# Moving the order of work inside a fused attention and FFN kernel: first pair's sums, next x's second half, y's turn, one maximum, one pair's statistics

## The chip, the cores and the metric

The kernel runs on one core of a Trainium2 chip. The metric is device time in microseconds (us). A core has five engines that run beside each other, each in the order in which its instructions were written: TensorE (PE in the profile, with its weight loads as PEld), VectorE (DVE), ScalarE (ACT), GpSimd (POOL) and SyncE (SP), which here only issues transfers. An engine that waits for something holds up all that stands behind it in its own list.

## The reference

Eight items (B = 8) of 1024 rows and 256 columns pass through one block. `mod` holds six rows for each item, and the two gates are kept away from zero.

```python
h = layernorm(x) * (1 + ca) + sa
x = x + ga * attention(h)            # softmax(h*w_lhs @ (h*w_rhs).T) @ h
h = layernorm(x) * (1 + cb) + sb
x = x + gb * (relu(h @ W1 + b1) @ W2 + b2)
```

All of it is float32. The scores of an item are symmetric (each is a sum over columns of x, x and both weights), so the kernel computes those on and above the diagonal and turns the rest.

## The kernel before, in words

The outer loop runs over items `b`, the inner one over eight steps `i`; step i belongs to row tile i of 128 rows. While attention runs for item b, the FFN of item b - 1 is interleaved: half 0 (`fg` = 0) in steps 0 to 3, half 1 in steps 4 to 7. A half has 512 rows. Its first matmuls are taken in four "pairs" c = 0 to 3, two in steps 0 and 1 (4 and 5) each, its second matmuls in steps 2 and 3 (6 and 7). Both products are done by a Strassen-like scheme with seven products instead of eight, so there are sums before and after them on DVE and POOL. `pin` (L63) ties each engine to the order in which the program was written: a statement's place in the loop is its place in every engine's list. DMAs are issued from SP's list, but for the loads of x and of two rows, which are issued from ACT's.

What each step issues, as far as the change touches it:

- `direct` (L403) makes the scores of row tile i + 2 on PE, copied to `sc` by ACT; `mirror` (L424) turns them on DVE (`Tm`), writes them to HBM in four transfers (`D_m`) and reads them back into `sc` as the columns of the later tiles (`move`, L300). `row_max` (L461, DVE, reads all of a tile's scores) gives `m`; `max_turn` (L466, PE) spreads it as `pm`; `subtract` (L471, DVE) and `exponent` (L483, ACT) make `pT`.
- Two row tiles form a pair. `left_sums` (L563) makes four sums on POOL. `pair_begin` (L539) issues products on PE and a copy to `W` on ACT (one buffer), `pair_end` (L574) twenty more products, and `pair_out` (L594) eight instructions on DVE that read the PSUM tiles `pq` and `pr` and write x. `pair_stats` (L620) takes the two tiles' statistics.
- `pair_products` (L723) issues the FFN's first products `pa`, `pb`, `pc` and the ACT copy `kept`; `between` is called behind them. `pair_sums` (L749) is five DVE instructions (L757 to L767), `pair_last` (L769) one product, one DVE add (L775) and one POOL add (L776), `pair_relu` (L780) two ACT instructions, `pair_turn` (L787) four POOL instructions that make `ft`.
- `y_first` (L803) issues `ya` and `yb`. Their first halves read `f`; then ACT copies `ya` to the tile `Y` (L811, one buffer), and the second half of `ya` follows on PE and reads `ft[:, 1]` of all four pairs. `y_second` (L825) issues `yc` and `yd`. `y_gate` scales Y on ACT, `y_turn` (L855) turns it with two DVE transposes (L860), writes four transfers `D_y` and leaves the reading back for later: the next `move` that is in a hurry or `y_add` (L868) issues it. `y_add` is two POOL adds (L873) of Y to x, and `y_out` (L875) writes x.
- `ffn_norm` (L643, ACT into `X_f`), `ffn_blocks` (L676, two DVE transposes, `D_f`, read back into X) and `ffn_turn` (L682) make the FFN's input `hT` and its sums `hs` on POOL.
- For the next item: `load_x`, `prepare_stats` (DVE), `prepare_rstd` (two ACT instructions), `prepare_norm` (one DVE, four ACT), `prepare_blocks` (two DVE transposes, `D_a`, read back into the single buffer `X`), `prepare_turn_apart` (L336, two ACT instructions for each side). `x_plus` and `xg_times` only append POOL work to a queue, which `spare()` takes from in steps 2, 3, 6 and 7.

In step 4 the order is: `direct`, `pair_begin`, pair 0 of the FFN with `max_turn` of tile 5 behind its products, `subtract` of tile 5, `y_turn`, `mirror` of tile 6, `pair_last`, pair 1 with `exponent` and `left_sums`, `prepare_norm` and `prepare_blocks` of the next item's second half, then `row_max` of tile 6. In step 5 pair 2 follows, with `max_turn` of tile 6 behind its products, then pair 3, `subtract` of tile 6, `y_add` and two `pair_turn`.

Of the kernel before, what the change touches and what calls it, by code (L numbers as in the profile page):

```python
# [24 lines left out]
def adaln_block_kernel(  # L25
# [14 lines left out]
    B, S, D = x.shape  # L40
# [228 lines left out]
    def prepare_rstd(b, g):  # L269
        pre[b, g].append(rstd_of(pre[b, g][0], "ra", f"ra_{b}_{g}"))  # L270
# [195 lines left out]
    def max_turn(b, i):  # L466
        pm = ps_t.tile([P, HALF], F32, tag="t", name=f"pm_{b}_{i}")
        nc.tensor.transpose(pm[:, :P], max_t.pop((b, i)).to_broadcast([P, P]), ident)
        pT_t[b, i] = pm
# [194 lines left out]
    def x_plus(b, g):  # L664

        for t in range(g * TH, (g + 1) * TH):
            xr = x_tile(b, t)
            later(xr, xr, rows_t[b][:, 1, :], ALU.add)
# [54 lines left out]
    def pair_products(b, g, c, between=None):  # L723

        if c == 0:
            ffn["f"] = two.tile([P, NI, HALF], F32, tag="f", name=f"f_{b}_{g}", bufs=1)
            if b < B - 1:
                ffn["ft"] = two.tile([P, 3, NH, H2], F32, tag="ft", name=f"ft_{b}_{g}", bufs=1)
        hT, hs = ffn["hT", g]
        n = ts(c, P)  # L730
        s1, a22 = (w1[:, k, ds((c + NH) * P, P)] for k in range(2))

        pool, tag = (ps_s, "s") if b == B - 1 else (ps_a, "a")
        pa = ps_a.tile([P, HALF], F32, tag="a", name=f"pa_{b}_{g}_{c}")
        pb = pool.tile([P, HALF], F32, tag=tag, name=f"pb_{b}_{g}_{c}")
        pc = ps_a.tile([P, HALF], F32, tag="a", name=f"pc_{b}_{g}_{c}")
        mm(pa[:, lo], w1[:, 0, n], hT[:, 0, lo])
        mm(pa[:, hi], s1, hs[:, 0])

        tag, bufs = ("s1", 1) if b == B - 1 and c % 3 == 2 else ("kept", 2)  # L740
        kept = work.tile([P, HALF], F32, tag=tag, name=f"kept_{b}_{g}_{c}", bufs=bufs)
        nc.scalar.copy(kept, pa)  # L742
        mm(pb[:, lo], w1s[:, 0, n], hs[:, 1])
        mm(pb[:, hi], w1s[:, 1, n], hs[:, 2])
        mm(pc[:, lo], w1[:, 1, n], hT[:, 1, lo])
        mm(pc[:, hi], a22, hT[:, 0, hi])
        if between:
            between()
        pairs[c] = pa, pb, pc, kept  # L749
# [387 lines left out]
    def weights(b, i):  # L1137
        subtract(b, i)
        exponent(b, i)
# [3 lines left out]
    for b in range(B):  # L1143
        for i in range(NT):
# [6 lines left out]
            c = i % TH * 2  # L1151
# [56 lines left out]
            if first:  # L1208

                ub, ug = (b - 1, 0) if i >= TH else (b - 2, 1)  # L1210
                back = i % TH == 0 and ub >= 0
                returned = i % TH == 1 and ub >= 0
                if i == 4:
                    pair_begin(b, i)
                    pair_begin_sum(b, i)
                pair_products(fb, fg, c, turn_max)
                if i == 0:
                    ffn_rstd(b - 1, 1)
                if back:
                    y_gate(ub)  # L1220
                if i == 4:
                    if b + 1 < B:
                        prepare_rstd(b + 1, 1)
                if i % TH == 1:
                    pair_relu(c - 1)
                pair_sums(fb, fg, c)
                if (b, i) == (1, 0):
                    subtract(*late)
                elif i == 4:
                    subtract(*late)  # L1230
                if back:
                    y_turn(ub, ug)
                if ahead:
                    mirror(*ahead)
                if i == 1:
                    left_sums(b, 0)
                pair_last(fb, fg, c)
                if i % TH == 1:
                    pair_turn(c - 1)
                if (b, i) == (B - 1, 5):  # L1240
                    pair_stats(b, 2)
                pair_products(fb, fg, c + 1, (lambda: max_turn(*extra)) if extra else None)
                if (b, i) == (1, 0):
                    exponent(*late)
                    late = None
                if (b, i) == (B - 1, 5):
                    ffn_rstd(b, 0)
                if i == 4:
                    exponent(*late)
                    left_sums(b, i)  # L1250
                    if b + 1 < B:
                        prepare_norm(b + 1, 1)
                        x_plus(b + 1, 1)
                pair_relu(c)
                pair_sums(fb, fg, c + 1)
                pair_last(fb, fg, c + 1)
                if i == 0:
                    pair_begin(b, i)
                if late and i != 4:
                    weights(*late)  # L1260
                if i == 5 and b + 1 < B:
                    prepare_turn_apart(b + 1, 1, 1)
                    prepare_turn_apart(b + 1, 1, 0)
                middle(b, i)
                if i == 4 and b + 1 < B:
                    prepare_blocks(b + 1, 1)
                    xg_times(b + 1, 1)
                if ahead and ahead != extra:
                    row_max(*ahead)
                if returned:  # L1270
                    for q in range(2):
                        y_add(ub, ug, q)
                pair_turn(c)
                if c > 0:
                    pair_relu(c + 1)
                    pair_turn(c + 1)
            else:
                half = i % TH - 2
                if i == NT - 2 and b < B - 1:
                    pair_stats(b, 2)  # L1280
                if i == 2:
                    pair_begin(b, i)
                elif i == 3:
                    turn_max()
                elif i == 6:
                    pair_begin(b, i, lambda: (max_turn(*late), weights(*late)))
                else:
                    turn_max()
                    pair_end(b, i - 1)
                    if not ahead:  # L1290

                        pair_out(b, i - 1)
                        pair_stats(b, i - 1)
                if half:
                    y_second(fb, fg)
                else:
                    y_first(fb, fg, turn_max if i == 2 else None)
                if ahead:
                    mirror(*ahead)
                if i == 2 and b + 1 < B:  # L1300
                    prepare_rstd(b + 1, 0)
                elif i == 6 and b + 1 < B:
                    ffn_rstd(b, 0)
                elif i == NT - 1 and b == B - 1:
                    ffn_rstd(b, 1)
                if not half:
                    pair_begin_sum(b, i)
                    if i == 2:
                        weights(*late)
                    left_sums(b, i)  # L1310
                spare()
                early(b, i)
                if late and half:
                    weights(*late)
                middle(b, i)
                if i == 2 and b + 1 < B:
                    load_x(b + 1, 1)
                spare()
                if ahead:
                    row_max(*ahead)  # L1320
                if half:
                    if i == NT - 1 and ahead:
                        pair_out(b, i - 1)
                    y_second_sums(fb)
                    if i == NT - 1 and b == B - 1:
                        y_gate(fb)
                    elif i == 3:
                        pair_stats(b, 0)
                        if b + 1 < B:
                            prepare_stats(b + 1, 1)  # L1330
                else:
                    y_first_sums()
                    if i == NT - 2:
                        pair_stats(b, 4)
                spare()
            if extra:
                subtract(*extra)
            if i == NT - 1 and 0 < b < B - 1:
                while queue:
                    spare()  # L1340
                right_sums(b + 1, range(4))
            turns(b, i)
            norms(b, i)
            if extra:
# [3 lines left out]
                    spare()  # L1348
            if i == 0:
                pair_begin_sum(b, i)  # L1350
            elif i in (1, 3, 5):
                pair_end(b, i - 1)
                pair_out(b, i - 1)
                if i == 3 and b + 1 < B:
                    prepare_turn_apart(b + 1, 0, 1)
                    prepare_turn_apart(b + 1, 0, 0)
            elif i == NT - 1 and ahead:
                pair_stats(b, i - 1)
            late = ahead if ahead != extra else None
# [82 lines left out]
```

## Time and profile before

| | |
|---|---|
| three runs | 801.06, 804.87, 805.19 us, median 804.87 us |
| the profiled execution: its time, its span | 801.43 us, 799.3 us |
| mean granted TensorE clock | 0.996 |
| PE busy, share of the span | 758.0 us, 95% |
| DVE | 621.5 us, 78% |
| POOL | 577.4 us, 72% |
| ACT | 377.5 us, 47% |

The 2.1 us between time and span lie around the instructions. The view of waits lists, for an engine, which earlier instruction ended its idle time, with the total, the number of times and the longest. The timeline gives the start of a group of like instructions in us from the span's start, its length, engine, line, operation, operands and count, and in brackets the idle time before it and what ended it; a letter q behind the engine marks an issue of its queue. One item takes some 96 us; item 4's steps 4 to 7 lie at about 411 to 460 us.

### The profile page before, as it was taken

How to read it: one execution, taken by the hardware profiler on the slowest of the kernel's cores; microseconds unless marked ns; L12 is line 12 of the kernel's file. 1: busy time of each engine (PE TensorE's matmuls, PEld its weight loads, DVE VectorE, ACT ScalarE, POOL GpSimd, SP SyncE). 2: the span in 40 equal slices, each digit the busy share in tenths (PEclk: the TensorE clock that was granted, in tenths of full speed). 3: DMA queues.
4: the chain of work that ended last, by engine and by line, in shares of the span. 5: the costliest groups of instructions: out<-in, count | busy, mean ns of one | idle time of the engine just before them, and what ended most of it. 6: DMA issues, size and time to landing. Idle time of an engine off the chain costs nothing.

```text
span 799.3 us, 12434 instructions
## 1 busy us (share of the span) xinstructions
PE 758.0 (95%) x4044; PEld 624.8 (78%) x4044; DVE 621.5 (78%) x1358; ACT 377.5 (47%) x695; POOL 577.4 (72%) x686
## 2 busy tenths in 40 slices
PE   8999998999989999899998999989998999998998
PEld 4687876787867788687796877868877788877887
DVE  7896789778896887867888688877779868785833
ACT  4563536534455445544455355553546535243421
POOL 3854876969779597885869968688686987758730
PEclk9999999999999999999999999999999999999999
DMA  8033253344533444434534444335452443424130
GB/s 291 14 107 112 73 159 92 103 135 133 165 113 114 124 140 132 124 113 124 158 103 139 145 125 142 100 110 145 132 164 71 125 123 112 113 60 146 43 115 27
DMA packets 106217, 95.25 MB, mean 119 GB/s; under 512 B 29701, under 2 KB 98849, under 8 KB 106153
## 3 DMA queue, kind: packets, MB, share of 16 engines
q1 hardware_dynamic: 98408, 85.81, 36.6%
q10 hardware_dynamic: 7744, 8.65, 3.5%
q8 instruction: 32, 0.52, 0.3%
q14 instruction: 33, 0.26, 0.1%
HBM read 50.62 MB, written 43.81 MB: 118 GB/s over the span
## 4 chain that ended last, share of the span: by engine, by line
PE 71%; DVE 19%; issue 3%; ACT 3%; DMA 3%; DVEq 0%; SPq 0%; ACTq 0%
PE psc L412 13%; PE pr L588 7%; PE pa L721 6%; PE yc L799 6%; PE pb L721 5%; PE ya L799 5%; PE pq L588 5%; PE yb L799 5%; PE pp L549 4%; PE po L501 3%; PE py L909 3%; PE yd L799 3%; PE pc L721 3%; DVE u L767 2%; ACT X_f L653 2%
## 5 line engine op out<-in xcount | busy, mean ns | idle before, releaser
L412 PE MATMUL psc<-rT,lT 128*128 128x512 f32 (+3 forms) x384 | 134.8, 487 | 0.0
L484 ACT ACTIVATE pT<-pT 128x1024 f32<-128x1024 f32 x64 | 67.8, 1059 | 114.2 <-DVE pT L475 114.2
L776 POOL TENSOR_TENSOR f<-f,kept 128x256 f32<-128x256 f32 x64 | 49.3, 771 | 95.3 <-DVE f L766 74.4
L475 DVE TENSOR_TENSOR pT<-sc,pm 128x1024 f32<-128x1024 f32 x64 | 77.6, 1213 | 34.4 <-DMA sc<-D_m 19.7
L412 PEld LDWEIGHTS psc<-rT,lT 128*128 128x128 f32 x384 | 66.4, 191 | 37.3 <-issue 25.3
L463 DVE TENSOR_REDUCE m<-sc 128x1 f32<-128x1024 f32 x64 | 77.3, 1207 | 2.3 <-ACT sc L419 1.7
L419 ACT COPY sc<-psc 128x512 f32<-128x512 f32 (+3 forms) x96 | 44.1, 473 | 72.7 <-PE psc L412 58.6
L721 PE MATMUL pb<-hs,w1s 128*128 128x256 f32 x256 | 68.1, 390 | 3.1 <-DVE f L760 3.1
L721 PE MATMUL pc<-hT,w 128*128 128x256 f32 x256 | 66.9, 384 | 0.0
L549 PEld LDWEIGHTS pp<-xg,pT 128*128 128x128 f32 x448 | 54.3, 192 | 10.5 <-issue 4.8
L742 ACT COPY kept<-pa 128x512 f32<-128x512 f32 x64 | 37.5, 586 | 52.6 <-PE pa L721 52.5
L567 POOL TENSOR_TENSOR s<-pT 128x512 f32<-128x512 f32 x28 | 35.6, 1270 | 33.4 <-ACT pT L484 33.4
L588 PE MATMUL pq<-tsum,pT 128*128 128x128 f32 (+1 forms) x448 | 59.3, 275 | 0.3 <-DVE f L760 0.3
L721 PEld LDWEIGHTS pb<-hs,w1s 128*128 128x128 f32 x256 | 48.8, 194 | 12.7 <-DVE f L760 5.7
L549 PE MATMUL pp<-xg,pT 128*128 128x129 f32 x448 | 56.1, 277 | 1.0 <-ACT pT L484 0.2
L721 PEld LDWEIGHTS pc<-hT,w 128*128 128x128 f32 x256 | 49.6, 194 | 7.1
L757 DVE SCALAR_TENSOR_TENSOR u<-pb,cols,kept 128x256 f32<-128x256 f32 x64 | 30.4, 475 | 31.6 <-PE pb L721 26.4
L588 PEld LDWEIGHTS pq<-tsum,pT 128*128 128x128 f32 x448 | 54.5, 192 | 0.5 <-DVE f L760 0.5
L637 POOL TENSOR_TENSOR x<-x,rows 128x256 f32<-128x256 f32 x64 | 44.5, 726 | 12.7 <-ACT rows L1015 9.6
L782 ACT ACTIVATE f<-f 128x512 f32<-128x512 f32 x64 | 40.2, 628 | 22.7 <-DVE f L775 22.7
L799 PE MATMUL yc<-f,w2s 128*128 128x256 f32 x224 | 50.7, 379 | 0.0
L783 ACT ACTIVATE f<-f 128x512 f32<-128x512 f32 x64 | 39.7, 621 | 17.4 <-POOL f L776 17.3
(167 smaller groups left out, 1931.8 us busy)
## 6 DMA issues: line engine op xcount, KB each, us to landing
D_f<-T_f SPq DMA_DIRECT2D x60, 128.0 KB, 2.3
X_f<-D_f SPq DMA_DIRECT2D x15, 512.0 KB, 3.8
D_a<-T_a SPq DMA_DIRECT2D x56, 128.0 KB, 2.8
D_y<-T_y SPq DMA_DIRECT2D x56, 128.0 KB, 2.3
Y<-D_y SPq DMA_DIRECT2D x14, 512.0 KB, 4.3
out_dram<-x SPq DMA_DIRECT2D x14, 512.0 KB, 3.0
X_a<-D_a SPq DMA_DIRECT2D x13, 512.0 KB, 3.4
x<-in_L_attn_x_dram ACTq DMA_DIRECT2D x12, 512.0 KB, 3.8
```

What stands on the lines that cost most here:

```text
L412: nc.tensor.matmul(psc[:, : hi - lo], lhsT=lT_t[b, i // TH][:, k, ts(i % TH, P)], rhs=rT_t[b, n][:, k, lo - n * HALF : HALF], start=(k == ...
L419: nc.scalar.copy(score_row(b, i)[:, lo // V : hi // V, :], psc[:, : hi - lo].rearrange("p (n v) -> p n v", v=V),)
L463: nc.vector.tensor_reduce(m, score_row(b, i), AX.XY, ALU.max)
L475: nc.vector.tensor_tensor(pT.rearrange("p j (a v) -> p j a v", v=V), score_columns(b, i), pm[:, :P].rearrange("p (j a v) -> p j a v", j=1, ...
L484: nc.scalar.activation(pT_t[b, i], pT_t[b, i], AF.Exp)
L549: nc.tensor.matmul(out, lhsT=lhs[:, t, :], rhs=xg_t[b][:, h * TH + t, P : P + XS], start=(t == 0), stop=(t == TH - 1),)
L588: nc.tensor.matmul(out, lhsT=lhs[:, t, :], rhs=rhs[:, t, :], start=(t == 0), stop=(t == TH - 1),)
L637: queue.append(lambda: nc.gpsimd.tensor_tensor(out, in0, row, op))
L721: nc.tensor.matmul(out, lhsT=lhsT, rhs=rhs, start=True, stop=True)
L776: nc.gpsimd.tensor_tensor(f[:, c + NH, hi], f[:, c + NH, hi], kept[:, hi], ALU.add)
L782: nc.scalar.activation(f[:, c, :], f[:, c, :], AF.Relu)
L799: nc.tensor.matmul(out, lhsT=lhs(c), rhs=rhs(c), start=(c == 0), stop=(c == NH - 1))
```

## The change

The diff moves calls inside the loop; no function's body changes. In step 1 `pair_end` and `pair_out` of the first pair stand in front of `turns` and `norms` instead of behind them (`norms` of step 1 issues `ffn_blocks`, `prepare_start` and `prepare_stats`). The next item's second half has its statistics, `prepare_rstd`, `prepare_norm`, `x_plus`, `prepare_blocks` and `xg_times` in step 3 instead of steps 3 and 4, its `load_x` in step 2 ahead of `prepare_norm` of the first half; `prepare_turn_apart` of the first half stays in step 3 and now stands ahead of these blocks. The y of steps 4 and 5 is turned in step 5, behind `subtract` and `exponent` of tile 6; that of steps 0 and 1 is left where it was. The maximum of tile 6 is spread behind pair 3's products instead of pair 2's. `pair_stats` of the first pair goes from step 3 to step 6, but for the last item.

```diff
--- before.py
+++ after.py
@@ -1213,14 +1213,11 @@
                 if i == 4:
                     pair_begin(b, i)
                     pair_begin_sum(b, i)
-                pair_products(fb, fg, c, turn_max)
+                pair_products(fb, fg, c, turn_max if i != 5 else None)
                 if i == 0:
                     ffn_rstd(b - 1, 1)
                 if back:
                     y_gate(ub)
-                if i == 4:
-                    if b + 1 < B:
-                        prepare_rstd(b + 1, 1)
                 if i % TH == 1:
                     pair_relu(c - 1)
                 pair_sums(fb, fg, c)
@@ -1228,7 +1225,7 @@
                     subtract(*late)
                 elif i == 4:
                     subtract(*late)
-                if back:
+                if back and i == 0:
                     y_turn(ub, ug)
                 if ahead:
                     mirror(*ahead)
@@ -1239,7 +1236,10 @@
                     pair_turn(c - 1)
                 if (b, i) == (B - 1, 5):
                     pair_stats(b, 2)
-                pair_products(fb, fg, c + 1, (lambda: max_turn(*extra)) if extra else None)
+                pair_products(
+                    fb, fg, c + 1,
+                    turn_max if i == 5 else (lambda: max_turn(*extra)) if extra else None,
+                )
                 if (b, i) == (1, 0):
                     exponent(*late)
                     late = None
@@ -1248,9 +1248,6 @@
                 if i == 4:
                     exponent(*late)
                     left_sums(b, i)
-                    if b + 1 < B:
-                        prepare_norm(b + 1, 1)
-                        x_plus(b + 1, 1)
                 pair_relu(c)
                 pair_sums(fb, fg, c + 1)
                 pair_last(fb, fg, c + 1)
@@ -1258,13 +1255,12 @@
                     pair_begin(b, i)
                 if late and i != 4:
                     weights(*late)
+                if i == 5:
+                    y_turn(ub, ug)
                 if i == 5 and b + 1 < B:
                     prepare_turn_apart(b + 1, 1, 1)
                     prepare_turn_apart(b + 1, 1, 0)
                 middle(b, i)
-                if i == 4 and b + 1 < B:
-                    prepare_blocks(b + 1, 1)
-                    xg_times(b + 1, 1)
                 if ahead and ahead != extra:
                     row_max(*ahead)
                 if returned:
@@ -1295,8 +1291,13 @@
                     y_second(fb, fg)
                 else:
                     y_first(fb, fg, turn_max if i == 2 else None)
+                if i == 6 and b + 1 < B:
+                    pair_stats(b, 0)
                 if ahead:
                     mirror(*ahead)
+                if i == 3 and b + 1 < B:
+                    prepare_stats(b + 1, 1)
+                    prepare_rstd(b + 1, 1)
                 if i == 2 and b + 1 < B:
                     prepare_rstd(b + 1, 0)
                 elif i == 6 and b + 1 < B:
@@ -1308,13 +1309,16 @@
                     if i == 2:
                         weights(*late)
                     left_sums(b, i)
+                if i == 2 and b + 1 < B:
+                    load_x(b + 1, 1)
                 spare()
                 early(b, i)
                 if late and half:
                     weights(*late)
+                if i == 3 and b + 1 < B:
+                    prepare_norm(b + 1, 1)
+                    x_plus(b + 1, 1)
                 middle(b, i)
-                if i == 2 and b + 1 < B:
-                    load_x(b + 1, 1)
                 spare()
                 if ahead:
                     row_max(*ahead)
@@ -1325,9 +1329,13 @@
                     if i == NT - 1 and b == B - 1:
                         y_gate(fb)
                     elif i == 3:
-                        pair_stats(b, 0)
                         if b + 1 < B:
-                            prepare_stats(b + 1, 1)
+                            prepare_turn_apart(b + 1, 0, 1)
+                            prepare_turn_apart(b + 1, 0, 0)
+                            prepare_blocks(b + 1, 1)
+                            xg_times(b + 1, 1)
+                        else:
+                            pair_stats(b, 0)
                 else:
                     y_first_sums()
                     if i == NT - 2:
@@ -1339,6 +1347,9 @@
                 while queue:
                     spare()
                 right_sums(b + 1, range(4))
+            if i == 1:
+                pair_end(b, 0)
+                pair_out(b, 0)
             turns(b, i)
             norms(b, i)
             if extra:
@@ -1348,12 +1359,9 @@
                     spare()
             if i == 0:
                 pair_begin_sum(b, i)
-            elif i in (1, 3, 5):
+            elif i in (3, 5):
                 pair_end(b, i - 1)
                 pair_out(b, i - 1)
-                if i == 3 and b + 1 < B:
-                    prepare_turn_apart(b + 1, 0, 1)
-                    prepare_turn_apart(b + 1, 0, 0)
             elif i == NT - 1 and ahead:
                 pair_stats(b, i - 1)
             late = ahead if ahead != extra else None
```

## The prediction

> **What bounds the kernel now.** I read the page first (PE 95% busy, all others at 78% or less), then what PE waits for, then the timeline of item 4's steps 4 to 6, engine by engine. In the view of waits the five costliest rows of PE, from 40 us on, are
>
> ```profile
> PE pm L468 <- DVE m L463: 18.6, 7, 2.9
> PE yb L799 <- DVE pr L606: 7.0, 7, 1.7
> PE pb L721 <- DVE f L760: 3.1, 6, 0.5
> PE ya L799 <- ACT Y L811: 2.8, 2, 2.6
> PE pa L721 <- DVE f L775: 2.4, 7, 0.5
> ```
>
> Their sum, 33.9 us, is the most that any reordering can win: 4.2% of the span, some 5 us of an item's 96. Two places in an item carry it. In the timeline of PE they are, step 5 first and step 2 of the next item second:
>
> ```profile
> 420.22 0.70 PE L721 MATMUL pa<-hT,w 128*128 128x256 f32 x2 [0.41 <-DVE f L775]
> 421.87 1.13 PE L721 MATMUL pb<-hs,w1s 128*128 128x256 f32 x4 [0.52 <-DVE f L760]
> 426.76 0.32 PE L468 MATMUL pm<-ident,m 128*128 128x128 f32 x1 [2.90 <-DVE m L463]
> ...
> 489.91 1.99 PE L799 MATMUL yb<-f,w 128*128 128x256 f32 x8 [0.98 <-DVE pr L606]
> ```
>
> In step 5 DVE is late: from 415.2 to 434.4 it is never idle, and these three of its rows stand in front of tile 6's maximum:
>
> ```profile
> 418.36 1.29 DVE L860 STREAM_TRANSPOSE T_y<-Y 128x512 f32<-128x512 f32 x2
> 420.09 0.81 DVE L277 SCALAR_TENSOR_TENSOR rs<-mva,ra 128x4 f32<-128x4 f32 x1
> 424.31 1.29 DVE L322 STREAM_TRANSPOSE T_a<-xg 128x512 f32<-128x512 f32 x2
> ```
>
> **First pair's sums earlier: -1.5 us an item.** In item 4's step 2, `yb` waits for L606, since `pair_out` began at 392.42, behind T_f (389.09, after 1.40 idle) and four pairs of statistics (2.1). Moved ahead, it starts when the maximum ends (387.7) and `pair_end`'s last product is through (387.4), and ends 2.7 later at 390.4. `yb` then follows `ya` at 390.72 + 1.73 = 392.45, not 393.60, and the second half of `ya` starts at 394.3, not 395.79: L811 was queued behind the copy to W, which waited 4.63 for `pair_out` and now doesn't. Together 1.5. The price: T_f ends 1.3 later, and its X_f read goes to SP at 395.35, not 394.04; `y_out` and tile 4's mirror stand behind it, so its writes start at 396.2, not 395.63. hT has its cover until pair 0 in step 4.
>
> **Next x's second half earlier, a pair's statistics later.** From step 4 go one small DVE row (0.7 in place), T_a (1.2) and four ACT rows (2.1). Into step 3 come the same; there DVE idled 1.81 ahead of `subtract` of tile 4, and the 2.1 of x's statistics fill that gap. `pair_stats` (1.06) leaves step 3 and lands in step 6 behind `subtract` of tile 7, where DVE idled 1.19 at the next mirror. `load_x` now stands on ACT ahead of the four `prepare_norm`, and its buffer must have been written out: `y_out` at 395.75 plus 3.0 (its median landing) is 398.8, so ACT stands 2 us. That keeps T_a of step 2 where it was in absolute time (about 401). The D_a transfers move past tile 6's mirror, into a stretch in which SP idled from 411.1 to 419.7; POOL's queued x and xg rows are the same eight and still run in steps 6 and 7. I cost this at nothing by itself. Bounds: -0.5 an item if DVE reaches pair 0 earlier, +0.7 if the x load slows the mirror's transfers.
>
> What it does to `subtract` of tile 5 (417.23), where the next chain begins: `subtract` of tile 4 waits for its mirror, 404.44 + 0.6 = 405.0. Then 1.15 for it, 1.05 exponent, 2.1 for four norms, 1.25 T_a, 2.7 `pair_out`, 0.85 for W and `kept`, 2.05 for five sums: 416.15. So of the 1.5 gained, 1.1 arrives.
>
> **Maximum and y later: the stall of 3.8 goes.** Without T_y, T_a and the small row in front of it, tile 6's maximum ends near 421.8, and its `pm` is now asked for behind pair 3's products, near 424.8. 2.90 + 0.52 + 0.41 = 3.83 goes. All that stands between is 3 us of cover.
>
> **What is late next.** `y_turn` now stands behind `subtract` of tile 6, and `y_add` in the same step needs its data back from HBM. Before, Y was asked for at 426.12 and the adds ran at 433.37 without a wait; these are POOL's rows, and everything under L873 is queued behind it:
>
> ```profile
> 424.96 0.72 POOL L776 TENSOR_TENSOR f<-f,kept 128x256 f32<-128x256 f32 x1
> ...
> 432.69 0.73 POOL L776 TENSOR_TENSOR f<-f,kept 128x256 f32<-128x256 f32 x1
> 433.37 2.51 POOL L873 TENSOR_TENSOR x<-x,Y 128x512 f32<-128x512 f32 x2
> ...
> 439.35 0.73 POOL L792 TENSOR_TENSOR ft<-f 128x256 f32<-128x256 f32 x1 [0.48 <-ACT f L783]
> 440.16 0.73 POOL L793 TENSOR_TENSOR ft<-ft,f 128x256 f32<-128x256 f32 x1
> ```
>
> PE's second half of `ya` (443.63) needs the last of these. From `subtract` of tile 5 I count: POOL's L776 of pair 1 ends 8.45 later (425.68 - 417.23; exponent and four left sums are in it). ACT's second relu of pair 1 waits for that, and `kept` of pair 3 is behind it: 1.15. Five sums and L775 of pair 3: 2.6 (429.40 to 431.98). `subtract` of tile 6: 1.13. T_y: 1.3. Its transfers: the shortest stretches from the first of four writes to the read's issue are 3.6 to 3.7 (390.43 to 394.04, 725.23 to 728.95), and from a read to its first user 3.4 to 3.6 (X_a 431.89 to 435.31, 406.29 to 409.85); I take 7.0. `y_add` 2.5, `pair_turn` of pair 2 3.05, two rows of pair 3's 1.55, PE's last two records 0.45. Sum 29.2: the second half of `ya` would end at 416.15 + 29.2 = 445.35. Before it ended at 443.63 + 1.73 = 445.36.
>
> So POOL stands idle some 6 us where it had no wait, PE waits there in turn, and the 5.3 gained is paid back: without new waits `ya` would end at 440.0. L811, too, must wait for `y_add`, since Y has one buffer (about 440.3); `load_x` behind it on ACT waits for `y_out` (near 443.5), and `ffn_norm` starts about when it did (444.29), so X_f and hT are covered as before. `left_sums` of tile 6's pair start about 4 later and end 451.8; `pair_end` needs the last of them near 453.9. Per item: 0.0, for six items nothing.
>
> **The last item** prepares nothing, so less was late: PE waited 1.18 + 0.26 in step 5. The same sum from 705.8 (its old 705.94: the mirror's 0.6 eats the 1.5) goes through DVE, which was the later there: T_y ends at 720.6, Y is back at 727.6, `ya` ends at 727.6 + 2.5 + 3.05 + 1.55 + 0.45 = 735.15 instead of 732.62. Its left sums then end 1.1 too late for `pair_end`: +3.6.
>
> **The clock.** After the 2.90 of items 3 and 5 the granted clock was 0.50 and four `pb` records took 1.91 instead of 1.03; after item 4's it stayed at 1.00. From step 4's `pair_begin` to the next item's those two stretches took 97.8 instead of 96.3: 3.0 in all. They go. The new wait has a longest gap of 2.4 (between the two pair_turns); at two in six or fewer I charge one such loss, 1.5.
>
> The Trainium skill, "TensorE: Matmul & The Clock Gate", section "Why this matters for your kernels", advises no idle gaps over some 3 us, as one idle window drops the clock to half. The rows show the drop after 2.90. By the page the new gap is safe, and the sum would be 1.5 lower.
>
> **Sum.** 0.0 + 3.6 - 3.0 + 1.5 = +2.1 on the profiled execution's 801.43. That lies 3.4 below the median of 804.87; on the median it is 807.0, and I say 807: nothing that can be told.
>
> The skill's "DMA: Bandwidth & Descriptors", section "Anatomy of one DMA", would put a transfer at 2.0 us plus bytes over 436 GB/s. My estimate by that page for 128 KB and 512 KB is 2.3 + 3.2 = 5.5, not the rows' 7.0; seven items would then gain 10 and the time would be 797.
>
> **Rivals.** *Faster*: the chain from `subtract` of tile 5 is shorter than 29.2. The tile arrives at PE's pace (415.7: -0.45), the transfers at the shortest rows (6.9: -0.1), DVE's rows unstretched beside an idle POOL (-0.6): -1.2 an item, -8 in seven, 799. It is decided by Y's add starting before 437.5 in item 4's frame; every us earlier is worth 7, until at -5.3 an item all stalls are gone (770), for which no row speaks.
>
> *Slower*: Y comes back later, and each us costs 7. The one place where y was asked for at once, in the tail, speaks for it:
>
> ```profile
> 757.66 1.98 SPq L306 DMA_DIRECT2D D_y<-T_y  x4
> 762.29 0.34 SPq L309 DMA_DIRECT2D Y<-D_y  x1
> ...
> 765.60 2.49 POOL L873 TENSOR_TENSOR x<-x,Y 128x512 f32<-128x512 f32 x2 [5.70 <-DMA Y<-D_y]
> ```
>
> 7.94 instead of 7.0, beside another read; with 0.7 for the x load against the mirror, +1.6 an item, 818. It decides from an add after 438.5. Against it: no other transfer is issued in that stretch.
>
> *Nothing moved*: tile 6's maximum is still last, or PE's gain of step 2 alone is left: 803 to 807.
>
> **Chances.** Forecast 0.45 (803 to 811; 0.28 of it within half a per cent, 0.16 slower, 0.01 faster). Faster rival 0.32 (0.29 and 0.03 within). Slower rival 0.19. Nothing moved 0.04. Half a per cent, 4 us, is what a measurement can tell from no change. So faster 0.30, same 0.35, slower 0.35. The range, 794 to 818, leaves out some 0.1 at each end.
>
> **What would show it.** PE's waits for m and for L606 gone from the list; a new wait of PE's `ya` for POOL's `ft` or ACT's Y, 4 to 5 us an item; a wait of L873 for Y of some 6; ACT standing at `load_x`. If `ya` of step 6 does not wait, the step "what is late next" is wrong, and the time is under 790. If `pm` still waits, the cover of 3 us is.

## The result, and the profile after

The changed kernel took 826.07 us in the median of four runs (825.37 to 827.8), the kernel before 803.93 (801.06 to 805.19, four runs): a ratio of 1.0284, 95% interval 1.025 to 1.0318. The change costs 22 us. The forecast was 807.0 with a range of 794 to 818, so it is outside, on the slow side. The profiled execution took 825.37 us, 1.8 of them around its span. Of its page, the span, the engines' busy time and the shares of the chain that ended last:

```profile
span 823.6 us, 12454 instructions
...
PE 768.8 (93%) x4044; PEld 624.6 (76%) x4044; DVE 620.1 (75%) x1358; ACT 378.6 (46%) x695; POOL 579.4 (70%) x686
...
PE 36%; DVE 22%; POOL 18%; DMA 13%; issue 6%; ACT 3%; SPq 1%; DVEq 0%; POOLq 0%; ACTq 0%
```

DVE, POOL and ACT have no more to do than before (DVE 620.1 against 621.5 us, POOL 579.4 against 577.4). PE has the same 4044 records and is busy 10.8 us longer: by the record of the granted clock 17.1 us lie at half the clock, before 6.8, and a record behind a wait takes longer (two records of `ya` 0.70 us, without a wait 0.59). PE's waits from 40 us on grow from 34.4 to 47.7 us. What is new is the chain: before it ran through PE for 71% of the span, now for 36%, and POOL and transfers have 31%. What PE waits for, from 40 us on (total, times, longest):

```profile
PE ya L799 <- POOL ft L793: 14.9, 7, 2.3
PE ya L799 <- ACT Y L811: 9.9, 7, 4.0
PE pa L721 <- ACT kept L742: 8.1, 7, 1.2
PE pp L549 <- DVE Y L843: 6.7, 6, 2.4
PE pb L721 <- DVE f L760: 3.3, 6, 0.6
PE pb L721 <- POOL hs L711: 2.7, 4, 0.7
```

The two old rows at the top are gone, `pm` for `m` (18.6) and, but for one wait of 0.4, `yb` for L606 (7.0). Six others have come or grown, and they sum to 45.6.

The item is easiest to read in four sections, from the first `pp` record of `pair_begin` in one even step to the next. Medians over five items of the profiled executions, worked out from the starts in PE's timeline; "item" is the mean of six whole items, "last" runs from the last item's step 0 to the end:

| us | 0 to 2 | 2 to 4 | 4 to 6 | 6 to next 0 | item | last |
|---|---|---|---|---|---|---|
| before | 16.4 | 22.3 | 27.0 | 30.6 | 97.0 | 136.3 |
| after | 16.4 | 21.9 | 25.6 | 35.8 | 100.1 | 141.8 |

The change wins 0.4 and 1.4 where it was to win, and loses 5.2 in steps 6 and 7. Span: six items at 3.1, 5.5 in the last, 0.3 ahead of the first, 24.3 together. Now item 4. PE's timeline, start and length:

```profile
420.00 2.02 PE L549 MATMUL pp<-xg,pT 128*128 128x129 f32 x16 [1.01 <-DVE Y L843]
...
452.00 1.78 PE L799 MATMUL ya<-ft,w2s 128*128 128x256 f32 x6 [0.88 <-ACT Y L811]
456.05 0.70 PE L799 MATMUL ya<-ft,w2s 128*128 128x256 f32 x2 [2.27 <-POOL ft L793]
456.59 2.82 PE L799 MATMUL yb<-ft,w 128*128 128x256 f32 x8
```

POOL in the same stretch:

```profile
442.78 0.73 POOL L776 TENSOR_TENSOR f<-f,kept 128x256 f32<-128x256 f32 x1
449.04 2.50 POOL L873 TENSOR_TENSOR x<-x,Y 128x512 f32<-128x512 f32 x2 [5.53 <-DMA Y<-D_y]
...
455.27 0.72 POOL L793 TENSOR_TENSOR ft<-ft,f 128x256 f32<-128x256 f32 x1
```

And SP's issues behind it, T_y's four writes and the read:

```profile
442.14 1.76 SPq L306 DMA_DIRECT2D D_y<-T_y  x4
445.77 0.34 SPq L309 DMA_DIRECT2D Y<-D_y  x1
```

POOL has nothing to do from 443.5 on and stands 5.53 us at the head of its list for Y's way through HBM (442.14 to 449.04, 6.9 us). Eight `pair_turn` rows are queued behind the two adds, and PE's second half of `ya` needs one of the last of them (L793 at 455.27). This is the picture that the forecast drew. Why it costs 22 us, and not nothing, is what the runs are for.

### The profile page after: what moved, and what is told of

It reads as the page before. It is cut to its first block, busy times and chain, and to the rows that moved or that the text cites. A ratio compares the mean times of both kernels' runs of the same rounds, so it can differ in the third digit from the quotient of the medians.

```text
span 823.6 us, 12454 instructions
## 1 busy us (share of the span) xinstructions
PE 768.8 (93%) x4044; PEld 624.6 (76%) x4044; DVE 620.1 (75%) x1358; ACT 378.6 (46%) x695; POOL 579.4 (70%) x686
## 4 chain that ended last, share of the span: by engine, by line
PE 36%; DVE 22%; POOL 18%; DMA 13%; issue 6%; ACT 3%; SPq 1%; DVEq 0%; POOLq 0%; ACTq 0%
PE psc L412 7%; PE pa L721 4%; PE pb L721 4%; PE po L501 3%; PE py L909 3%; DMA out_dram<-x 3%; DMA Y<-D_y 3%; DVE pT L475 3%; POOL tsum L534 3%; PE pp L549 2%; PE pc L721 2%; DMA x<-in_L_attn_x_dram 2%; POOL x L873 2%; POOL pT L571 2%; POOL pT L572 2%
## 5 line engine op out<-in xcount | busy, mean ns | idle before, releaser
L873 POOL TENSOR_TENSOR x<-x,Y 128x512 f32<-128x512 f32 x28 | 35.1, 1274 | 45.7 <-DMA Y<-D_y 45.7
L783 ACT ACTIVATE f<-f 128x512 f32<-128x512 f32 x64 | 39.8, 622 | 51.1 <-POOL f L776 51.1
L799 PE MATMUL ya<-ft,w2s 128*128 128x256 f32 x112 | 32.6, 420 | 24.8 <-POOL ft L793 14.9
```

What stands on the lines that cost most here:

```text
L799: nc.tensor.matmul(out, lhsT=lhs(c), rhs=rhs(c), start=(c == 0), stop=(c == NH - 1))
L873: nc.gpsimd.tensor_tensor(x2, x2, y, ALU.add)
```

## The experiments

**The theory after the result.** y's turn behind `subtract` of tile 6 makes a chain (T_y, HBM, two adds, eight POOL rows) that ends later than PE would arrive, and all that the rest of the change wins in front of it is lost at it. It should go if y alone is put back. **The rivals.** The loss lies in steps 2 and 3, where x is stored, loaded and normalized in one row (`y_out` late, ACT held at `load_x`); or in the clock, which fell to half in more places. The diffs of the first five are against the changed kernel, those of the single edits against the kernel before; each ratio is against the kernel before on the same chip. The changed kernel was not run again beside them: differences from it are by the medians here, and by the ratios they come out 2 to 3 us larger.

### y back in step 4

```diff
-                if back and i == 0:
+                if back:
                     y_turn(ub, ug)
...
-                if i == 5:
-                    y_turn(ub, ug)
```

> The changed kernel with y of steps 4 and 5 turned in step 4 again. Theory 1 (two costs: y's return from HBM in step 5, and x's load that stands on ACT in step 2 until x was written out, which starts step 5's chain 2.0 us later): PE's waits for ft and for L811 in step 6 go, 0.88 + 2.27 an item in item 4, and most of the half-rate clock windows behind them; 1.16 for kept stays. 826 - 22 - 6 = 798. Rival A (y's return is all of the cost, the wait for the load has cover): the other moves then bring their full 5.3 an item, 770 to 785. Rival B (the load is all, PE would wait for something else in step 6): 818 to 826.

Measured: 792.95 us, ratio 0.9844 (0.9819 to 0.9869), 5 under the theory's 798 and above the 770 to 785 of rival A. By the medians the one call costs 33 us inside the change, and the rest of the change is faster than the kernel before. Sections 16.4, 22.0, 25.5, 30.9: steps 6 and 7 cost 5 less, and steps 4 and 5 take 25.5 against 25.6. So y's departure from step 4 won nothing there: x's second half had left DVE enough room already. PE's waits in this kernel:

```profile
PE pp L549 <- DVE Y L843: 7.9, 6, 3.1
PE pa L721 <- DVE f L775: 5.3, 7, 0.8
PE pb L721 <- DVE f L760: 5.2, 7, 0.8
PE ya L799 <- ACT Y L811: 2.6, 1, 2.6
```

### x written out ahead of the sums

```diff
+            if first and returned and i == 1:
+                y_out(ub, ug)
             if i == 1:
                 pair_end(b, 0)
                 pair_out(b, 0)
...
-            if first and returned:
+            if first and returned and i != 1:
                 y_out(ub, ug)
```

> The changed kernel with y_out of step 1 ahead of the FFN input's turns on SP, so that x's buffer is free sooner. Theory 1: ACT's wait of 4.4 us at load_x goes, tile 4's and tile 5's subtract start 2.0 to 2.7 us sooner against PE's pair_begin of step 2, and as the chain behind it stays 29.2 long, the second half of ya moves by the same: six items, 826 - 12 to 16 = 810 to 814. Rival A: the wait has cover, 824 to 828. Rival B: all that was lost comes back, 800 or less.

Measured: 819.83 us, ratio 1.0176 (1.0148 to 1.0204): the direction, not the size. What was to move did. In the changed kernel SP issues the store of x behind X_f's read and in front of the mirror's four writes, and ACT, which issues `load_x` into that buffer, waits for it to land:

```profile
404.56 0.34 SPq L309 DMA_DIRECT2D X_f<-D_f  x1
404.94 0.43 SPq L876 DMA_DIRECT2D out_dram<-x  x1
405.42 3.76 SPq L306 DMA_DIRECT2D D_m<-Tm  x4
```

```profile
410.02 0.37 ACTq L86 DMA_DIRECT2D x<-in_L_attn_x_dram  x1
410.45 2.08 ACT L281 ACTIVATE xg<-x,rs,ra 128x256 f32<-128x256 f32 x4 [4.42 <-DMA out_dram<-x]
```

With the store earlier the same rows of ACT, in this run's item 4, follow each other without a wait:

```profile
402.46 1.06 ACT L484 ACTIVATE pT<-pT 128x1024 f32<-128x1024 f32 x1 [1.37 <-DVE pT L475]
402.52 0.37 ACTq L86 DMA_DIRECT2D x<-in_L_attn_x_dram  x1
403.43 2.06 ACT L281 ACTIVATE xg<-x,rs,ra 128x256 f32<-128x256 f32 x4
```

From step 2's `pair_begin` (398.11 and 395.59) the four norms begin 7.84 later instead of 12.34, and `subtract` of tile 5 comes at 27.59 instead of 29.23; the forecast had 27.21. Sections 2 to 4 and 4 to 6 are 21.9 to 20.7 and 25.6 to 25.4 (25.1 in two items), 1.3 to 1.7 less. But steps 6 and 7 take 36.3, 0.5 more: the chain through Y is what PE now meets sooner, and in every item the granted clock falls to half behind it. Windows of this run (PEclk is the third figure from the right):

```profile
450.00:453.00 3.00, 1.13 (x5) 1.03 (x6) 0.39 (x1) 2.00 (x4) 2.84 (x5) 1.00 0.85 227
453.30:456.50 3.20, 3.20 (x8) 2.15 (x7) 1.17 (x4) 0.00 (x0) 3.04 (x4) 0.50 0.67 198
457.00:460.00 3.00, 3.00 (x16) 1.88 (x15) 1.78 (x4) 1.07 (x2) 2.92 (x5) 1.00 0.22 54
```

So the rival's loss is real: by the medians 6 of the 22 us. The other rival, the clock, is not the cause: this run has 27.3 us at half the clock where the changed kernel has 17.1, and it is the faster of the two.

### POOL's order in step 5: y added behind the turns

```diff
-                if returned:
+                if returned and i == 1:
                     for q in range(2):
                         y_add(ub, ug, q)
+                if i == 5:
+                    read_back()
                 pair_turn(c)
                 if c > 0:
                     pair_relu(c + 1)
                     pair_turn(c + 1)
+                if i == 5:
+                    for q in range(2):
+                        y_add(ub, ug, q)
```

> The changed kernel with the two y_add of step 5 behind both pair_turn on POOL; Y's read is issued where it was. If POOL's order is what turns Y's way back into PE's wait, ft is there in time, and the second half of ya waits for L811 alone (y_add ends some 1.1 us later than PE comes): 3.2 of the 4.2 of waiting in step 6 go and with them the half-rate windows: 826 - 6 x 3.6 - 4 = 800. Rival (Y's way back itself, through its one buffer): PE waits for L811 nearly as long as for ft, 818 to 826.

Measured: 800.62 us, ratio 0.9926 (0.9901 to 0.9951), as expected. y is still turned in step 5; only the eight `ft` rows no longer stand behind the adds. PE's wait for `ft` is gone, its second half of `ya` is one group of eight, and what stays is ACT's copy into Y, which has to wait until the adds have read it:

```profile
441.89 1.99 PE L799 MATMUL ya<-ft,w2s 128*128 128x256 f32 x8 [1.35 <-ACT Y L811]
```

25 us of the 33 come by way of the place of two instructions in POOL's list; y's late turn costs them only through that.

### Both costs away

y back in step 4 and `y_out` ahead of the sums, the two diffs above together.

> The changed kernel with y turned in step 4 and y_out of step 1 ahead of the FFN input's turns: both costs taken away. Theory 1: step 2 to step 4 takes 20.7 us an item (as with the early y_out alone) instead of 21.9, step 4 to 6 25.1 instead of 25.5, the rest stays: 793 - 6 x 1.6 = 783. Rival (with y in step 4 the load's wait has cover): 791 to 795.

Measured: 783.25 us, ratio 0.9724 (0.9701 to 0.9748), as expected: faster than both kernels. Sections 16.4, 20.7, 25.1, 30.9. Of PE's waits, the 7.9 for Y with y in step 4 alone has fallen to 1.1. Its largest are DVE's and short, 5.3 for L775 and 5.2 for L760 with none over 0.8; the longest single one, 2.6 for ACT's L811, is in the last item.

### The sums taken back as well

y in step 4, and `pair_end` and `pair_out` of the first pair behind `norms`, as before (`elif i in (1, 3, 5)`).

> The changed kernel with y turned in step 4 and the first pair's sums where they were. Alone, those sums cost 13 us. Theory 1: with DVE relieved in step 4 they gain what PE waited for L606 less what x's load takes, 0.4 an item; without them PE waits 1.5 in step 2 again, but x is written out sooner and steps 4 and 5 lose 1.0 less: 788 to 796. Rival (the sums are worth 1.5 an item once DVE is relieved): 803.

Measured: 783.9 us, ratio 0.9731 (0.971 to 0.9751): 4 us under the expectation. Beside 792.95 with the sums in front, they cost 9 us where `y_out` stands behind them. The sums in front together with the early store (783.25) are worth no more than neither of the two; the early store without the sums was not run, so what each is worth there is not shown. The starts say how, counted from step 2's `pair_begin` of item 4: the norms begin at 10.94 without them and 12.49 with them, `subtract` of tile 5 at 28.16 and 29.38. The first pair's sums push T_f, so X_f's read and `y_out`, by 1.3 (the store is issued at 6.83 with them and at 5.49 without), as forecast; from there it goes through `load_x` and the norms on to DVE.

### Each edit alone, on the kernel before

The sums:

```diff
+            if i == 1:
+                pair_end(b, 0)
+                pair_out(b, 0)
             turns(b, i)
...
-            elif i in (1, 3, 5):
+            elif i in (3, 5):
```

> The kernel before with the first pair's sums alone moved. My forecast charged -1.5 us an item to it. Theory 1: PE's second half of ya in step 2 comes 1.5 sooner, but DVE's row up to tile 6's maximum doesn't (subtract of tile 4 waits for its mirror, which is written 0.3 to 0.6 later), so the wait for the maximum in step 5 grows from 2.9 to 4.4 or more and takes it back: 802 to 808. Rival: the gain is its own, 804 - 10 = 794.

Measured: 817.96 us, ratio 1.0158 (1.0125 to 1.0192), a miss of 10. Section 2 to 4 falls from 22.3 to 20.7, the 1.5 of the forecast. Section 4 to 6 rises from 27.0 to 31.3. PE comes to step 4 sooner, and DVE doesn't: six pairs of statistics (415.02 to 418.2) stand in front of the second pair's `pair_out`. PE in item 4:

```profile
419.48 1.10 PE L721 MATMUL pb<-hs,w1s 128*128 128x256 f32 x4 [1.28 <-DVE pr L606]
...
427.09 0.70 PE L721 MATMUL pa<-hT,w 128*128 128x256 f32 x2 [0.84 <-DVE f L775]
...
428.73 1.13 PE L721 MATMUL pb<-hs,w1s 128*128 128x256 f32 x4 [0.52 <-DVE f L760]
...
433.63 0.47 PE L468 MATMUL pm<-ident,m 128*128 128x128 f32 x1 [2.90 <-DVE m L463]
433.89 1.06 PE L721 MATMUL pa<-hT,w1s 128*128 128x256 f32 x2
```

So the gain is paid back at the next thing that DVE owes; that was expected. The rest goes with the clock (PE is busy 7.0 us longer): behind the 2.90 two `pa` records took 1.06 instead of 0.59, and the trace has six windows of 3.4 us at half the clock (two pairs of them joined) where the kernel before has two.

y alone:

```diff
-                if back:
+                if back and i == 0:
                     y_turn(ub, ug)
...
+                if i == 5:
+                    y_turn(ub, ug)
```

> The kernel before with y's turn alone moved from step 4 to step 5. Theory 1: DVE gets 1.2 back in front of the maximum (its wait falls from 2.9 to some 1.7), but y_add has to wait for Y, and from subtract of tile 5 to the end of the second half of ya it is 29 to 30 us, where it was 28.1: +1 to +2 an item and +3.6 in the last, 814 to 820. Rival (y's return costs only beside the other moves): 796 to 804.

Measured: 820.51 us, ratio 1.019 (1.0158 to 1.0221), half a us over the expected range. Section 4 to 6 falls to 24.2, and 6 to next 0 rises to 36.1. PE's first rows:

```profile
PE ya L799 <- POOL ft L793: 15.7, 7, 2.3
PE pm L468 <- DVE m L463: 9.9, 7, 1.7
PE ya L799 <- ACT Y L811: 9.8, 8, 3.9
```

The maximum alone (both `turn_max` edits of step 5):

> The kernel before with the maximum of tile 6 alone spread behind pair 3's products. DVE's row isn't shortened, so PE's wait goes from the maximum to the PSUM buffers of pair 3 (L760) and what follows: 0.4 an item gained, and the half-rate windows go as no single wait is 2.9 long: 796 to 800. Rival (the maximum's place was the whole wait): 804 - 7 x 2.9 = 784.

Measured: 798.79 us, ratio 0.9917 (0.9897 to 0.9936), as expected. The 18.6 for `m` go, those for L760 grow from 3.1 to 12.2, and 5.2 for `kept` come; one half-rate window is left, in the last item.

Next x's second half alone (`load_x`, `prepare_stats`, `prepare_rstd`, `prepare_norm`, `x_plus`, `prepare_blocks`, `xg_times` and the first half's `prepare_turn_apart` as in the change; `pair_stats` stays in step 3):

> The kernel before with the next x's second half alone prepared a step sooner. T_a and the small row (1.9 us) leave DVE's row in front of tile 6's maximum in step 4; in step 3 the statistics fill DVE's wait for the mirror, T_a delays the second pair's sums by some 0.3. The wait for the maximum falls from 2.9 to some 1.3 and the half-rate windows go: 804 - 9 - 3 = 792. Rival (what leaves step 4 delays step 3 by as much): 800 to 806.

Measured: 787.57 us, ratio 0.9778 (0.9751 to 0.9805): more than expected. Section 4 to 6 is 24.9, and no half-rate window falls on the loop (mean clock 1.000). The wait for `m` shrinks from 2.90 to

```profile
415.91 0.32 PE L468 MATMUL pm<-ident,m 128*128 128x128 f32 x1 [1.11 <-DVE m L463]
```

The statistics alone (`pair_stats` of the first pair in step 6):

> The kernel before with the first pair's statistics alone in step 6. DVE begins the second pair's sums 1.06 sooner in step 3, but in step 4 it waits for PE's pb of pair 0 anyway, so 0.1 to 0.2 an item arrives at the maximum; in step 6 the 1.06 lie in a wait of 1.2: 801 to 805. Rival (DVE's row is one chain from step 3 on): 804 - 7 = 797.

Measured: 805.32 us, ratio 1.0001 (0.9989 to 1.0012): nothing, as expected.

Against their own runs of the kernel before, the five edits alone give +12.9, +15.5, -6.6, -18.2 and -0.4: +3 in sum, and +22 together. They don't add. y's move costs 15.5 alone and 33 beside the others: alone it also takes 2.8 an item from section 4 to 6 (27.0 to 24.2, the wait for `m` from 18.6 to 9.9), beside the others nothing (25.5 to 25.6), since they had removed that wait.

## Why the prediction was wrong, point by point

In the frame of item 4's step 2 (`pair_begin` at 388.94 before, 398.11 after), the steps stand so:

| | before | forecast | after |
|---|---|---|---|
| `subtract` of tile 5 | 28.29 | 27.21 | 29.23 |
| from it to the end of the second half of `ya` | 28.1 | 29.2 | 29.25 |
| from there to the next item's `pair_begin` | 23.50 | 23.5 | 24.7 |

The second row of the column "after" is 456.59, where `yb` starts, less 427.34; the last is the value of items 3 and 6, which have no half-rate window there.

- **First pair's sums, -1.5: right, then lost.** `yb` no longer waits, and the second half of `ya` starts 5.35 behind `pair_begin` in place of 6.85. That 1.1 of it arrives at `subtract` of tile 5 did not hold: it comes 0.9 later than before instead.
- **"ACT stands 2 us": the step that failed first.** `y_out` was issued where the forecast put it (6.83 behind `pair_begin`; forecast 6.81). It was given its median landing of 3.0. The kernel before already had the right figure: its view of transfers, asked for step 2 alone, gives 5.0 for both stores there whose landing is recorded (items 2 and 6, issued at 200.4 and 588.6); the 3.0 are stores issued elsewhere. The critical view of the changed kernel shows what it took, between X_f's read of 512 KB, issued 0.38 ahead, and the mirror's four writes, issued 0.48 behind:

```profile
404.94 5.01 DMA out_dram<-x
410.02 3.16 DMA x<-in_L_attn_x_dram
```

- ACT stood 4.42. T_a, the mirror and the statistics are behind that on DVE, and `subtract` of tile 5 is 2.0 late. Moving the store confirmed it: 27.59. Two us in each of items 2 to 6 (item 1 has no store there) are 10; with them the forecast's own sum would have been 817. Of these 10 the early store gave back 6: items 2 to 5 are 1.0 to 1.8 shorter with it, but items 1 and 6 are 0.5 and 0.9 longer, and why they are stays open.
- **Next x's second half "at nothing by itself": wrong as an account.** Alone it is worth 18 us. The forecast booked T_a and the small row (2.1 of DVE) under the wait of 3.83 that the maximum and y were to remove. x alone brings section 4 to 6 to 24.9 and y alone to 24.2, so after the one nothing was left for the other.
- **"The stall of 3.8 goes": right for `pm`.** But `pa` now waits 1.16 for `kept`, `pb` 0.54, and `pb` and `pc` of pair 0 start 0.7 later, so 1.4 of it arrived in section 4 to 6.
- **What is late next, 29.2: right.** 29.25, and its parts with it: 14.8 up to T_y's first write (forecast 14.6), Y's own way 6.9 (7.0), 7.55 from the add on (7.55); POOL waited 5.53 for "some 6".
- **"X_f and hT are covered as before": wrong, 1.2 an item.** POOL made up in steps 6 and 7 what it had stood idle. In the kernel before, POOL was idle for 2.22 ahead of the sums `hs` of the next item:

```profile
457.54 1.27 POOL L534 TENSOR_TENSOR tsum<-tsum,xg 128x512 f32<-128x512 f32 x1
461.03 0.73 POOL L709 TENSOR_TENSOR hs<-hT 128x256 f32<-128x256 f32 x1 [2.22 <-DVE hT L700]
```

- In the changed kernel, one item earlier, it is never idle there, and PE waits for the third sum:

```profile
372.49 1.45 POOL L534 TENSOR_TENSOR tsum<-tsum,xg 128x512 f32<-128x512 f32 x1
373.90 0.72 POOL L709 TENSOR_TENSOR hs<-hT 128x256 f32<-128x256 f32 x1
```

```profile
376.04 1.13 PE L721 MATMUL pb<-hs,w1s 128*128 128x256 f32 x4 [0.67 <-POOL hs L711]
```

- **The clock, -3.0 + 1.5: about right.** Items 3 and 6 of the changed kernel take 99.6; the excess of items 2, 4 and 5 over it is 1.8, 0.8 and 0.4, some 3. But 1.4 of the 1.8 lie ahead of item 2's half-rate window: there `pp` waits 2.4 for Y instead of 1.0, because T_f's write landed in 3.74 instead of 2.24, the store behind it was issued 8.41 behind `pair_begin` instead of 6.83, and the norms waited 5.83 instead of 4.42.
- **The last item, +3.6: 5.5.** Same chain, and a window of 6.8 us at half the clock behind a wait of 3.98 for L811.

The sum, then: 2.0 in each of five items for the store; 1.2 in all six at `hs`; 0.8 more in the first; nothing for the clock and item 2's wait together (3 gone, 3 come) instead of -1.5; 5.5 in the last instead of 3.6: 23.5 instead of 2.1, of the 24.3 measured in the span. The step that failed is the store's landing, 3.0 assumed and 5.0 measured: 10 of the 21 us that the forecast's sum lacked follow from it, and 7 from the wait at `hs` that it put at nothing. The slower rival had the sign and +1.6 an item, but not the mechanism: Y did not come back later than assumed, the chain to it began later. Its own threshold, an add after 438.5 in the old frame, was passed: 449.04 less the 9.17 by which step 2 lies later is 439.87.

The Trainium skill, "DMA: Bandwidth & Descriptors", section "Anatomy of one DMA — SWDGE (gpsimd) path", gives 2.0 us plus bytes over 436 GB/s, fitted to DMAs issued on the gpsimd path; these transfers are issued by SP. My estimate by it for a 512 KB store is 3.2, which is near the median landing of 3.1 on the page of the changed kernel, and 1.8 under the 5.01 measured beside other transfers. For Y's way the estimate was 5.5, and it took 6.9.

## What to carry to other kernels

A transfer that is asked for and used within one step puts its whole way on whatever in-order list its user stands in (here Y 5.53 us of POOL's, the store 4.42 of ACT's): put work that others wait for ahead of that user, and date it from the landing beside the transfers really in flight, not from a median over all places. A gain in front of a fixed chain is only a longer wait at it, and two edits that remove the same wait do not add: try each alone and each left out before paying for all. Here the change without y's move, and with the store ahead of the sums, gave 783.25 us (ratio 0.9724), while the whole gave 826.07; next x's second half alone gave 787.57.

## What was not expected of the hardware

The half-rate clock follows shorter waits than thought. In item 4 of the changed kernel the longest gap was 2.27, with 0.88 a little ahead of it, and the clock was 0.50 for the next 3.4 us (PEclk, third figure from the right):

```profile
453.00:457.00 4.00, 1.73 (x7) 1.17 (x7) 1.39 (x3) 1.83 (x4) 3.76 (x7) 1.00 0.89 261
457.40:460.80 3.40, 3.40 (x8) 2.37 (x8) 1.32 (x5) 0.00 (x0) 3.24 (x4) 0.50 0.59 189
461.00:465.00 4.00, 4.00 (x24) 2.86 (x23) 2.72 (x6) 1.07 (x2) 3.92 (x6) 1.00 0.37 91
```

The Trainium skill, "TensorE: Matmul & The Clock Gate", section "Why this matters for your kernels", warns of gaps over some 3 us; here 2.27 was enough in item 4 and, with the same two waits (0.96 and 2.27 at 352 to 356), not in item 3, so the length of one gap doesn't decide it.

The record of the granted clock in the traces shows what does. All half-rate windows in the loop last 3.41 us or twice that, and in each of the twelve traces that has several they begin whole multiples of 3.413 us apart: 57 times in the kernel before (329.75 and 524.31), 69, 29 and 57 times in the changed one (221.87, 457.39, 556.38, 750.94). So the clock goes by a grid. Cut the traces into its stretches and sum PE's busy time in each (the ends of PE's records are modelled):

| stretch of 3.41 us | PE busy, us | clock in the next |
|---|---|---|
| changed kernel, item 4: 453.98 to 457.39 | 1.34 | half |
| changed kernel, item 3: 351.58 to 354.99, and the next | 1.78, 1.94 | full |
| before, item 3: 326.34 to 329.75 | 0.98 | half |
| before, item 4: 421.91 to 425.33, and the next | 1.95, 1.98 | full |
| before, item 5: 520.90 to 524.31 | 1.39 | half |

The same two waits fall into one stretch in item 4 of the changed kernel and into two in item 3; the wait of 2.90 of the kernel before falls into two in item 4. Over all twelve traces, of the stretches at full clock, all 30 with PE busy 1.41 us or less have half the clock behind them, none of the 2709 over 1.62 has, and of the 15 between 5 have. By these counts it is the idle time summed over a stretch that decides, some 2 us of 3.4, and so also where on the grid it falls.

Where a window falls in each item, they begin 99.0 us apart, 29 times 3.413: in the run with the early store at 156.2, 255.2, 354.2 and on to 651.2, in y alone at 254.4, 353.3 and on to 650.3. It looks as if the loop falls into step with the grid; no run tests that. Whether an item's length is held by it, and what share of the loss it has beside the waits themselves, stays open. A further buffer for x, which would free ACT of its wait at `load_x`, was not tried.
